# Layer 0's row sums folded into partition halves by DMA, and six graphs in the schedule instead of five

## The chip, the cores and the metric

The kernel runs on one core of one Trainium2 chip. The metric is the device time of one launch in microseconds. Engines are named as in the profile: PE is TensorE's matmul (PEld its weight load), DVE VectorE, ACT ScalarE, POOL GpSimd, SP SyncE. Each engine runs its own instructions in order and waits for others by semaphores; DMAs are issued from SP and from POOL.

## The reference

The input is 32 independent graphs of 512 nodes with 256 features (x is 32 x 512 x 256 in float32) and one 512 x 512 adjacency matrix. Four layers follow each other, each as `x = layernorm(x + layer(x))`:

- Layer 0: self-attention with 8 heads of 32 features, masked by the adjacency, then residual, layernorm, a two-product MLP with ReLU, residual and layernorm.
- Layer 1: graph attention with one head; the score is a leaky ReLU of a sum of a source and a target term.
- Layer 2: full attention with learned projections and a leaky ReLU on the scores, then ReLU.
- Layer 3: graph attention with 4 heads of 64 features, then ELU.

What matters here is the softmax of layer 0:

```
scores = einsum('fnhd,fmhd->fhnm', q, k) / sqrt(D)
scores = where(mask, scores, -1e9)
attn = softmax(scores, axis=-1)
t = einsum('fhnm,fmhd->fnhd', attn, v).reshape(F, N, C)
```

The kernel does not divide before the product with v: it computes the masked exponentials p, the product of p with v, and for each head and each node n the sum of p over m. The division comes after.

## The kernel before, in words

**Layout.** A tile of kind `p` is 128 partitions x 4 x 512 in float32 (8 KB per partition, 1 MB). In layer 0 the partitions are 128 of the 512 nodes m, the 4 parts are four heads (a head group), and the 512 columns are the nodes n. There are two head groups (g = 0, 1) and four node chunks (m = 0 to 3), so eight such tiles in each graph.

**Layer 0's attention (`layer0`, from L1046).** For each g and m: `exps` makes four score products that run on four row strips of TensorE (L1027) and four exponentials on ScalarE (L1031); VectorE multiplies by the mask (L1079); four products with v run on four column strips (L1086) and add up in one PSUM bank over m. `collect` (L1061 and after) sums the four chunks of a group outside TensorE: `add_dma` (L961 to L969) issues a DMA from POOL's queue that adds one tile to another in SBUF. For each group there are three: chunk 1 onto 0, chunk 3 onto 2, 2 onto 0. What is left is one tile for each group, kept in `totals`; its 128 partitions still have to be summed. `sums` (L1056, recorded at L1058) does it on TensorE: for each of the four parts a product whose stationary operand is `pick[:, g, :]`, a 128 x 32 tile that is zero but for a column g of ones. It runs on column strip j, so that row g of strip j of the bank `sm` becomes the row sum of head j of group g. The two groups take eight products. Each float32 product is two matmul instructions in the profile, so there are 16 for a graph. `rinv0` then moves `sm` back into columns and takes the reciprocal, and `heads_out` multiplies by it.

**Layer 3** does the same with four heads and its own sums (L1268); there `add_dma(total, None)` adds the second half of a tile's parts to the first. Its gates reach all partitions by way of DRAM: `gates` writes rows (L1173) and reads them back as a broadcast of 1 MB (L1179, `p<-row`) on SP's queue; layer 1 has a smaller one (`e<-row`). VectorE makes p from the broadcast at L1277 and masks it at L1284.

**The last graph** (`at_once`) takes the sums of all eight tiles on TensorE directly, without DMAs. `skip(n)` puts in n empty steps, so that every graph has the same number of steps.

**The schedule.** All 32 graphs are written as lists of steps (`plan(engine, ns, run, reads, writes, ...)`), each with an assumed duration. `Plan.place` (L521) then decides, in Python and before anything runs, in which order each engine issues the steps of all graphs: it keeps a clock for each engine, picks among the steps that are ready the one that can start first, and among those the one due first. A DMA's transfer is a step of a sixth engine, "DMA", with a `lag` until it has landed. The order is fixed in the program; at run time engines only wait for semaphores. What steers it:

- `WAYS`: a step of graph g may be placed only while g is less than WAYS past the oldest unfinished graph.
- `due` (L1351 and after): PACE times the graph's number plus a time from TENTHS (FIRST and LAST for the first four and last five graphs), by how far along the step is.
- `STAY`: a PE step whose mode of tiling differs from the last one's is treated as due later by this much. `tiling` is 1 for the row strips of the scores, 2 for the column strips of products with v and of sums, 3 for layer 3's products, 0 for the rest; `SWITCH` is the 100 ns that the planner charges for a change.
- `START`: the earliest time of the first graphs' first step.

Buffers are few and shared by all graphs (6 of kind x, 7 y, 3 v, 9 t, 8 p, 8 PSUM banks), and `place` gives them out as well.

Of the kernel before, what the change touches and what calls it, by code (L numbers as in the profile page):

```python
# [9 lines left out]
FP = mybir.dt.float32  # L10
# [7 lines left out]
P = 128  # L18
# [8 lines left out]
H0, H3 = 8, 4  # L27


WAYS = 5  # L30
PACE = 90.30
STAY = 4.86
START = (0, 0, 53.29, 88.61, 134.37)

TENTHS = (0, 26.21, 86.69, 92.24, 176.51, 212.02, 277.3, 313.49, 381.31, 382.21, 490.27)
FIRST = (
    (-14.58, 58.82, -25.93, -24.45, 99.53, 212.02, 277.3, 225.46, 380.43, 381.33, 489.39),
    (20.46, 79.82, -4.21, 95.49, 168.52, 212.02, 277.3, 315.61, 382.59, 384.58, 492.64),
    (10.74, 90.74, 6.57, 60.81, 176.51, 212.02, 277.3, 313.49, 383.92, 382.21, 492.29),
    (-115.77, 26.21, 86.69, 92.58, 176.51, 210.06, 277.3, 313.49, 381.31, 382.21, 487.12),)  # L40
LAST = (
    (0, 25.88, 86.52, 92.24, 176.3, 211.81, 277.09, 313.28, 381.68, 376.38, 536.57),
    (0, 27.77, 86.69, 92.22, 176.49, 212, 277.93, 316.39, 400.99, 521.01, 653.82),
    (0, 26.21, 87.61, 91.24, 177.97, 214.48, 309.58, 343.79, 765.5, 770.4, 888.75),
    (-0.65, 26.94, 85.87, 100.46, 141.72, 174.63, 259.04, 341.35, 397.71, 410.07, 514.93),
    (3.71, 25.72, 94.73, 50.65, 70.79, 101.96, 247.58, 292.79, 344.82, 346.48, 489.36),)
@with_exitstack
def general_path(
    ctx: ExitStack,
# [408 lines left out]
class Plan:  # L458
# [59 lines left out]
                live[slot.kind][r] += 1  # L518
        return live

    def place(self, urgency, ways, stay=0.0, run=True):  # L521


        held_by = {g: self.profile(g) for g in {op.graph for op in self.ops}}
        engines = {e: 0.0 for e in (PE, DVE, ACT, POOL, SP, DMA)}
        waiting = {e: [] for e in engines}
        free = {k: [(0.0, i) for i in range(n)] for k, n in self.counts.items()}
        todo, held = {}, {}
        for op in self.ops:
            todo.setdefault(op.graph, set()).add(op.rank)  # L530
            if not op.missing:
                waiting[op.engine].append(op)
        order, front, ended = sorted(todo), {g: 0 for g in todo}, {}
        port, port_by, end, tiling = 0.0, None, 0.0, 0
        self.trace = []

        def safe(op, kind, new):
            spare = len(free[kind]) - len(new)
            if spare < 0:
                return False  # L540
            have = spare
            for g in order:
                mine = held.get((g, kind), [])
                have += len(mine)
                if g == op.graph:
                    have += len(new)
                    mine = mine + new
                r, rows = front[g], held_by[g][kind]
                ahead = sorted(s.first for s in mine if s.first > r)
                for i, stop in enumerate(ahead + [len(rows)]):  # L550
                    if stop > r and max(rows[r:stop]) + len(ahead) - i > have:
                        return False
                    r = max(r, stop)
                if g == op.graph:
                    return True

        while todo:
            choice = None
            for e, ops in waiting.items():
                found = []  # L560
                for op in ops:
                    if order[0] + ways <= op.graph:
                        continue
                    due = urgency(op)
                    t = max(engines[e], op.ready, ended.get(op.graph - ways, 0.0))
                    if op.port and port_by is not e:
                        t = max(t, port)
                    if choice and t > choice[0]:
                        continue
                    wants = {}  # L570
                    for s in op.slots:
                        if s.index is None:
                            wants.setdefault(s.kind, []).append(s)
                    if all(safe(op, kind, new) for kind, new in wants.items()):
                        for kind, new in wants.items():
                            t = max(t, sorted(free[kind])[len(new) - 1][0])
                        if op.tiling != tiling and e is PE:
                            due += stay
                        found.append((t, due, op))
                if found:  # L580
                    best = min(found, key=lambda f: f[:2])
                    if choice is None or best[0] < choice[0]:
                        choice = best
            assert choice, "no instruction can be placed: too few buffers"
            t, _, op = choice
            if op.engine is PE and op.tiling != tiling:
                t, tiling = max(t, engines[PE] + SWITCH), op.tiling
            waiting[op.engine].remove(op)
            for s in op.slots:
                if s.index is None:  # L590
                    pick = min(free[s.kind])
                    free[s.kind].remove(pick)
                    s.index, s.graph = pick[1], op.graph
                    held.setdefault((op.graph, s.kind), []).append(s)
            engines[op.engine] = t + op.ns
            if op.port:
                port, port_by = t + op.ns, op.engine
            done = t + op.ns + op.lag + SIGNAL
            end = max(end, done)
            for s in op.slots:  # L600
                s.users -= 1
                s.ends = max(s.ends, done)
                if not s.users and s.kind:
                    free[s.kind].append((s.ends, s.index))
                    held[s.graph, s.kind].remove(s)
            for other in op.then:
                other.missing -= 1
                other.ready = max(other.ready, done if other.engine != op.engine or op.lag
                                  else t + op.ns)
                if not other.missing:  # L610
                    waiting[other.engine].append(other)
            left = todo[op.graph]
            left.remove(op.rank)
            while front[op.graph] not in left and left:
                front[op.graph] += 1
            ended[op.graph] = max(ended.get(op.graph, 0.0), t + op.ns + SIGNAL)
            if not left:
                del todo[op.graph]
                order.remove(op.graph)
            self.trace.append((t, op))  # L620
            if run and op.run:
                op.run()
        return end


def fast_path(
# [34 lines left out]
    nc = tc.nc  # L661
    B, N, C = x.shape
    NC = N // P
    KC = C // P
# [28 lines left out]
    ones = const.tile([P, P], FP, name="ones")  # L693
    nc.gpsimd.memset(ones, 1.0)

    pick = const.tile([P, 2, 32], FP, name="pick")
    nc.gpsimd.memset(pick, 0.0)
    for g in range(2):
        nc.gpsimd.memset(pick[:, g, g:g + 1], 1.0)


    fit = const.tile([P, NC * H0], FP, name="fit")
# [13 lines left out]
    def T(slot):  # L716
        return slot.tile if slot.kind is None else buffers[slot.kind][slot.index]
# [240 lines left out]
            [(s, c) for s in (a, b) if s is not None for c in (c0, c0 + 1)] + [row] * (row is not None),  # L958
            [(dst, c0), (dst, c0 + 1)])

    def add_dma(dst, src):  # L961

        def run():
            a, b = (T(dst), T(src)) if src else (T(dst)[:, 0:2, :], T(dst)[:, 2:4, :])
            nc.gpsimd.dma_start(a, b, accum_op=ALU.add)  # L965
        reads = [src, dst] if src else [dst]
        started = Slot(None)
        plan(POOL, 950, run, reads, [dst, started])
        plan(DMA, 5600 if src else 2650, None, reads + [started], [dst], lag=2500)  # L969
# [71 lines left out]
    def skip(n):  # L1041

        for _ in range(n):
            plan(DMA, 0, None)

    def layer0(xs, at_once):  # L1046
# [9 lines left out]
        def sums(g, p, start, stop):  # L1056
            for j in range(J):
                nc.tensor.matmul(T(sm)[j * 32:(j + 1) * 32, :], pick[:, g, :], T(p)[:, j, :],  # L1058
                                 start=start, stop=stop)
# [35 lines left out]
            totals.append(ps[0])  # L1095

        if at_once:
            skip(1)
        else:
            plan(PE, 1740, lambda: [sums(g, p, g == 0, g == KC - 1) for g, p in enumerate(totals)],  # L1100
                 totals, [sm], tiling=2)
        rinv = rinv0(sm)
        t = heads_out(oT, rinv, H0)

# [261 lines left out]
    with tc.manual_schedule(engines={mybir.EngineType.PE, mybir.EngineType.DVE,  # L1366
                                     mybir.EngineType.Activation, mybir.EngineType.Pool,
                                     mybir.EngineType.SP}):
        plan.place(urgency, WAYS, 1e3 * STAY)


    bad, col, total = buffers["rs"][:3]
# [51 lines left out]
```

## Time and profile before

The time is 2933.48 us, the median of three runs (2933.24 to 2937.47). The profiled execution has a span of 2933.2 us.

| what | value |
|---|---|
| TensorE (PE) | 2860.7 us busy, 98%, 14262 instructions |
| VectorE (DVE) | 2290.8 us, 78% |
| ScalarE (ACT) | 1888.0 us, 64% |
| GpSimd (POOL) | 953.7 us, 33% |
| DMA, POOL's queue | 292.57 MB, 49.7% of 16 engines |
| DMA, SP's queue | 80.49 MB, 9.0% of 16 engines |
| L1058, row sums of layer 0 | 560 instructions, 68.0 us busy |
| L965, accumulating DMAs | 310 issues, mean 882 ns each |

How to read it: the share is busy time over the span. A matmul's duration in the profile runs from its start to its modelled end, and several are in flight at a time, so the distance from one start to the next says more than the duration. In a group's line `out<-in` are the program's names, x is the count, then come the busy time and the mean of one, and last the idle time just before with what ended it. "Granted clock" is the share of TensorE's full clock.

### The profile page before, as it was taken

The numbers are of one execution on the slowest core, as the hardware profiler recorded it, in microseconds if no ns is written. First come the engines' busy times: TensorE is split into PE (matmuls) and PEld (weight loads), VectorE is DVE, ScalarE is ACT, GpSimd is POOL, SyncE is SP. The second block draws the span as 40 slices with busy tenths as digits, with TensorE's granted clock in tenths as the row PEclk, the third lists the DMA queues.
The fourth block names the chain that finished last, engine by engine and source line by source line (L and its number), as shares of the span: only waits on it lengthen the run. The fifth ranks groups of instructions, "written<-read, shape, count | busy, mean of one in ns | idle before, by whom it ended". The sixth has DMA issues, their size and how long they took to land.

```text
span 2933.2 us, 39746 instructions
## 1 busy us (share of the span) xinstructions
PE 2860.7 (98%) x14262; PEld 1586.7 (54%) x14262; DVE 2290.8 (78%) x4076; ACT 1888.0 (64%) x4104; POOL 953.7 (33%) x898
## 2 busy tenths in 40 slices
PE   8999999999999999999999999999999999999995
PEld 3455555555555555555555555555555555555572
DVE  5568887887878878778887778878778888777877
ACT  5665676666766667666667666667666667666653
POOL 0332233322333323433233343233433232333222
PEclk9999999999999999999999999999999999999998
DMA  6646665566655657556666556666556666555125
GB/s 164 133 83 137 132 132 125 110 150 135 143 122 110 148 126 151 119 113 139 141 147 142 128 115 137 143 145 140 130 115 137 143 145 139 131 113 125 48 59 126
DMA packets 93707, 375.66 MB, mean 128 GB/s; under 512 B 8768, under 2 KB 44736, under 8 KB 57664
## 3 DMA queue, kind: packets, MB, share of 16 engines
q0 software_dynamic: 44640, 292.57, 49.7%
q1 hardware_dynamic: 48864, 80.49, 9.0%
q8 instruction: 114, 1.87, 0.3%
q14 instruction: 89, 0.73, 0.1%
HBM read 63.38 MB, written 17.10 MB: 27 GB/s over the span
## 4 chain that ended last, share of the span: by engine, by line
PE 92%; DMA 3%; DVE 3%; ACT 1%; issue 1%; POOL 0%; DVEq 0%; SPq 0%; ACTq 0%
PE bank L924 15%; PE bank L910 11%; PE bank L1027 8%; PE bank L1086 8%; PE bank L1247 8%; PE bank L1293 8%; PE bank L1231 8%; PE bank L1208 8%; PE bank L897 5%; PE bank L1123 4%; PE bank L1135 3%; DMA p<-row 2%; PE bank L1058 2%; PE bank L1010 2%; DVE p L1079 1%; PE bank L978 1%
## 5 line engine op out<-in xcount | busy, mean ns | idle before, releaser
L965 POOL DMA_DIRECT2D p<-p x310 | 271.8, 882 | 1457.6 <-DMA p<-p 505.0
L1031 ACT ACTIVATE p<-bank 128x512 f32<-128x512 f32 x1024 | 546.7, 604 | 161.3 <-PE bank L1027 161.2
L1079 DVE TENSOR_TENSOR p<-p,edge_t 128x2048 f32<-128x2048 f32 x256 | 591.3, 2314 | 52.1 <-ACT p L1031 50.8
L885 ACT ACTIVATE t<-bank 128x512 f32<-128x512 f32 x640 | 369.1, 598 | 331.9 <-PE bank L1293 116.3
L955 POOL TENSOR_TENSOR y<-y,x 128x512 f32<-128x512 f32 x192 | 340.3, 1783 | 289.2 <-ACT y L1322 148.7
L938 DVE BATCH_NORM_STATS2 st<-y 128x6 f32<-128x256 f32 x768 | 314.0, 409 | 18.3 <-POOL y L955 11.5
L1086 PE MATMUL bank<-p,v 128*32 128x512 f32 x2048 | 277.3, 615 | 25.9 <-DVE p L1079 25.9
L1027 PE MATMUL bank<-t,t 32*128 32x512 f32 x2048 | 296.4, 643 | 0.0
L1284 DVE TENSOR_TENSOR p<-p,edge_t 128x2048 f32<-128x2048 f32 x128 | 293.1, 2290 | 3.3
L1277 DVE TENSOR_SCALAR p<-p,e,e 128x512 f32<-128x512 f32 x512 | 256.6, 545 | 36.4 <-DMA p<-row 36.0
L948 ACT ACTIVATE x<-y,rs,rs 128x256 f32<-128x256 f32 x512 | 270.9, 596 | 3.8 <-DVE rs L945 3.7
L1208 PE MATMUL bank<-v,p 128*128 128x257 f32 x1024 | 243.7, 385 | 3.5 <-issue 3.5
L910 PE MATMUL bank<-t,wqkv 128*128 128x512 f32 x512 | 240.7, 603 | 3.4 <-ACT t L885 3.3
L1247 PE MATMUL bank<-v,p 128*128 128x257 f32 x1024 | 242.3, 386 | 0.0
L1293 PE MATMUL bank<-p,v 128*64 128x512 f32 x1024 | 241.7, 613 | 0.5 <-DVE p L1284 0.5
L1231 PE MATMUL bank<-t,t 128*128 128x512 f32 x512 | 238.5, 599 | 0.0
L885 ACT ACTIVATE v<-bank 128x258 f32<-128x258 f32 (+2 forms) x384 | 172.1, 460 | 95.5 <-PE bank L924 92.8
L1247 PEld LDWEIGHTS bank<-v,p 128*128 128x128 f32 x1024 | 188.9, 190 | 64.5 <-ACT t L885 20.5
L1208 PEld LDWEIGHTS bank<-v,p 128*128 128x128 f32 x1024 | 190.3, 192 | 44.0 <-issue 18.2
L1027 PEld LDWEIGHTS bank<-t,t 32*128 32x128 f32 x2048 | 82.6, 184 | 163.3 <-issue 107.0
L939 DVE BATCH_NORM_AGGREGATE mv<-st 128x2 f32<-128x6 f32 x768 | 139.8, 182 | 26.3
L948 ACT ACTIVATE y<-y,rs,rs 128x256 f32<-128x256 f32 x256 | 140.0, 607 | 30.7 <-DVE rs L945 29.9
(120 smaller groups left out, 4167.3 us busy)
## 6 DMA issues: line engine op xcount, KB each, us to landing
p<-p POOLq DMA_DIRECT2D x248, 1024.0 KB, 7.5
p<-row SPq DMA_DIRECT2D x32, 1024.0 KB, 6.4
p<-p POOLq DMA_DIRECT2D x62, 512.0 KB, 4.6
x<-in_x_dram SPq DMA_DIRECT2D x32, 512.0 KB, 7.4
out_dram<-x SPq DMA_DIRECT2D x32, 512.0 KB, 2.9
e<-row SPq DMA_DIRECT2D x32, 256.0 KB, 3.1
t<-in_adj_dram SPq DMA_DIRECT2D x4, 256.0 KB, 6.2
wqkv<-in_L_gnn_w_qkv_dram SPq DMA_DIRECT2D x1, 768.0 KB
```

The costliest lines, as they stand in the source:

```text
L885: act(170 + n * 0.84, lambda: nc.scalar.activation(to(T(dst)), frm(T(src)), AF.Copy), [src], writes)
L910: nc.tensor.matmul(T(bank), T(w)[:, i, col:col + P], T(xT)[:, i, :], start=(i == 0), stop=(i == KC - 1))
L924: nc.tensor.matmul(T(bank)[:, j * width:(j + 1) * width], T(xT)[:, k, (c0 + j) * P:(c0 + j + 1) * P], T(w)[:, k, col:col + width], start=( ...
L948: act(600, lambda c=c: nc.scalar.activation(T(dst)[:, c, :], T(y)[:, c, :], AF.Identity, bias=T(nm)[:, c:c + 1], scale=T(rs)[:, c:c + 1]), ...
L1027: nc.tensor.matmul(T(banks[j]), T(kT)[r, g, m * P:(m + 1) * P], T(qT)[r, g, :], start=True, stop=True)
L1031: act(600, lambda j=j: nc.scalar.activation(T(p)[:, j, :], T(banks[j]), AF.Exp, scale=1.0 / math.sqrt(D0)), [banks[j]], [(p, j)])
L1079: dve(2420, lambda p=p, m=m: nc.vector.tensor_tensor(T(p), T(p), T(edge_t)[:, m, :].unsqueeze(1).to_broadcast([P, J, N]), ALU.mult), [p, ( ...
L1086: nc.tensor.matmul(T(av)[j * D0:(j + 1) * D0, :], T(v)[:, m, h * D0:(h + 1) * D0], T(p)[:, j, :], start=(m == 0), stop=(m == NC - 1))
L1208: nc.tensor.matmul(T(bank)[:, :C + 1], T(p)[:, m, c * P:(c + 1) * P], T(v)[:, m, 2:C + 3], start=(m == 0), stop=(m == NC - 1))
L1231: nc.tensor.matmul(T(bank), T(xT)[:, k, m * P:(m + 1) * P], T(qT)[:, k, :], start=(k == 0), stop=(k == KC - 1))
L1247: nc.tensor.matmul(T(bank)[:, :C + 1], T(p)[:, m, c * P:(c + 1) * P], T(v)[:, m, :C + 1], start=(m == 0), stop=(m == NC - 1))
L1293: nc.tensor.matmul(T(av)[i * D3:(i + 1) * D3, :], T(q)[:, m0 + m, 2 * H3 + h * D3:2 * H3 + (h + 1) * D3], T(p)[:, 2 * m + i, :], start=(m0 ...
```

## The change

It has two parts.

The first is in layer 0, for all graphs but the last. The two totals stay two tiles, `low` (group 0) and `high` (group 1). One accumulating DMA adds the upper 64 partitions of `low` to its lower 64, another adds the lower 64 partitions of `high` to its upper 64. Then a plain DMA on SP's queue copies the upper half of `high` to the upper half of `low`. `low` now has group 0 in partitions 0 to 63 and group 1 in 64 to 127. `pick` gets a third plane with ones in column 0 for the lower and in column 1 for the upper partitions, and four products with it (eight instructions) give the rows that eight products gave before. `skip(7)` replaces `skip(1)` for the last graph, because the other graphs now have six steps more.

The second is in the schedule: WAYS is 6 instead of 5, STAY is 0, PACE, START, TENTHS, FIRST and LAST have other values, and there is a new bound: no step may be placed earlier than EARLY (186.52 us) before it is due.

```diff
-WAYS = 5
-PACE = 90.30
-STAY = 4.86
-START = (0, 0, 53.29, 88.61, 134.37)
+WAYS = 6
+PACE = 81.87
+STAY = 0.00
+START = (0, 10.17, 59.24, 97.18, 85.64)
+EARLY = 186.52
...
-TENTHS = (0, 26.21, 86.69, 92.24, 176.51, 212.02, 277.3, 313.49, 381.31, 382.21, 490.27)
+TENTHS = (0, 35.72, 65.32, 68.92, 152.58, 202.32, 246.27, 266.73, 356.34, 362.66, 490.49)
...
                     t = max(engines[e], op.ready, ended.get(op.graph - ways, 0.0))
+                    if op.graph >= 0:
+                        t = max(t, due - early)
...
-    pick = const.tile([P, 2, 32], FP, name="pick")
+    pick = const.tile([P, 3, 32], FP, name="pick")
     nc.gpsimd.memset(pick, 0.0)
     for g in range(2):
         nc.gpsimd.memset(pick[:, g, g:g + 1], 1.0)
+        nc.gpsimd.memset(pick[g * 64:(g + 1) * 64, 2, g:g + 1], 1.0)
...
-    def add_dma(dst, src):
+    def add_dma(dst, src, halves=None):
...
-            a, b = (T(dst), T(src)) if src else (T(dst)[:, 0:2, :], T(dst)[:, 2:4, :])
+            a, b = (T(dst), T(src)) if src else halves(T(dst)) if halves else (
+                T(dst)[:, 0:2, :], T(dst)[:, 2:4, :])
...
         if at_once:
-            skip(1)
+            skip(7)
         else:
-            plan(PE, 1740, lambda: [sums(g, p, g == 0, g == KC - 1) for g, p in enumerate(totals)],
-                 totals, [sm], tiling=2)
+            low, high = totals
+            add_dma(low, None, lambda t: (t[:64], t[64:]))
+            add_dma(high, None, lambda t: (t[64:], t[:64]))
+            started = Slot(None)
+            plan(SP, 450, lambda: nc.sync.dma_start(T(low)[64:], T(high)[64:]), totals, [low, started])
+            plan(DMA, 1300, None, totals + [started], [low], lag=2500)
+            plan(PE, 870, lambda: sums(2, low, True, True), [low], [sm], tiling=2)
```

## The prediction

> **What bounds the kernel now.** I read the page from the top: busy shares, the chain of waits, then the costliest groups.
>
> ```profile
> span 2933.2 us, 39746 instructions
> PE 2860.7 (98%) x14262; PEld 1586.7 (54%) x14262; DVE 2290.8 (78%) x4076; ACT 1888.0 (64%) x4104; POOL 953.7 (33%) x898
> ...
> PE 92%; DMA 3%; DVE 3%; ACT 1%; issue 1%; POOL 0%; DVEq 0%; SPq 0%; ACTq 0%
> ```
>
> TensorE is busy for 98% of the span and is 92% of the chain that ended last; VectorE is next with 78%. So a product taken off TensorE counts, and work added elsewhere counts only where TensorE comes to wait for it. Is it equally full everywhere? I cut the run into two equal windows between start and tail, and added the two ends:
>
> ```profile
> 400.00:1400.00 1000.00, 981.02 (x4889) 543.81 (x4890) 785.58 (x1386) 651.97 (x1420) 341.41 (x312) 0.99 0.61 131
> 1400.00:2400.00 1000.00, 999.64 (x5017) 554.48 (x5016) 806.72 (x1423) 672.15 (x1464) 343.91 (x315) 1.00 0.63 137
> 0.00:200.00 200.00, 182.81 (x902) 90.01 (x903) 118.60 (x206) 116.44 (x235) 45.11 (x54) 0.96 0.61 134
> 2600.00:2933.00 333.00, 301.64 (x1474) 172.31 (x1470) 261.69 (x496) 191.62 (x425) 96.33 (x89) 0.96 0.40 92
> ```
>
> The second column is TensorE. The 14262 matmul instructions less 46 of set-up and check and 72 that the last graph has extra (64 instead of 16 row-sum instructions in layer 0, 32 instead of 8 in layer 3) are 442 per graph. So the first window does 4889/442 = 11.06 graphs, 90.4 us each; the second 11.35, 88.1 us each. The second window has no hole left: 88.1 us is what TensorE's own work takes. The first loses 2.3 us per graph; over the some 14 graphs that run before 1400 us that is 32 us. Start and tail leave TensorE idle for 17 and 31 us. The waits of TensorE and of VectorE say what makes the first window slower:
>
> ```profile
> PE bank L1086 <- DVE p L1079: 25.9, 13, 4.4
> PE bank L1380 <- DVE rs L1377: 11.3, 1, 11.3
> ...
> DVE p L1277 <- DMA p<-row: 36.0, 11, 6.2
> ```
>
> (Columns: total us, times, longest.) VectorE stands at L1277 for layer 3's gate broadcast (`p<-row`, 1 MB). Its queue is in order, the layer 0 mask L1079 is behind it, and TensorE's attention product L1086 waits for that mask. The timeline has this at 511 to 518 us and about every second graph up to 1260: that broadcast took 10.3 us beside two accumulating DMAs, TensorE waited 3.9 us, and the granted clock in the next 20 us was 0.93.
>
> Now the row sums themselves, in the stretch of the timeline around one of them:
>
> ```profile
> 1511.06 1.07 PE L1086 MATMUL bank<-p,v 128*32 128x512 f32 x8
> ...
> 1516.47 1.88 PE L1231 MATMUL bank<-t,t 128*128 128x512 f32 x4
> 1518.18 3.60 PE L910 MATMUL bank<-t,wqkv 128*128 128x512 f32 x8
> ...
> 1528.64 1.92 PE L1058 MATMUL bank<-p,pick 128*32 128x512 f32 x16
> 1530.49 1.98 PE L910 MATMUL bank<-t,wqkv 128*128 128x512 f32 x4
> ```
>
> Starts tell more than durations, which overlap. L1058 holds TensorE from 1528.64 to 1530.49: 1.85 us for 16 instructions, which run in four waves of four column strips. Four full instructions of L1231 take 1.71 us, 0.43 each; so a wave costs what one full instruction costs.
>
> [...] start to start, a 512-column instruction takes 429 ns inside a mode and 523 ns where the next is of another mode, so 94 ns per change (L1086's eight above: 1.00 us up to the next start at 1512.06, against two waves of 0.43). [...] No run here has a half-partition transfer[...]. [...] `p<-row` lands in 6.4 us by the median and in 10.3 beside two adds. [...]
>
> **The change, part by part.**
>
> *Row sums of layer 0.* For graphs 0 to 30, 16 instructions become 8: two waves fewer, 2 x 0.43 = 0.86 us, with the few ns between instructions 0.9. 31 x 0.9 = **28 us off TensorE**, in every window, because TensorE is the bound in all of them. The last graph takes its sums at once and keeps its 64.
>
> *The fold chain.* Each of those graphs gets two accumulating half-partition DMAs (512 KB) on POOL's queue and one SP copy (512 KB); the sums wait for the copy.
>
> ```profile
> p<-p POOLq DMA_DIRECT2D x248, 1024.0 KB, 7.5
> p<-p POOLq DMA_DIRECT2D x62, 512.0 KB, 4.6
> out_dram<-x SPq DMA_DIRECT2D x32, 512.0 KB, 2.9
> ```
>
> Fold: 4.6 us from issue to landing, if half the partitions cost nothing; at most 1.7 + 2 x 2.9 = 7.5 us, if the part that grows with size (7.5 - 4.6 = 2.9 us for 512 KB) doubles. Copy: 2.9 us by `out_dram<-x`[...]. In the stretch above the last add of that graph starts at 1517.5 and lands (by the median) at 1525.0; the sums start 3.6 us later. After the change: fold, 1529.6 to 1532.5; copy with 0.33 us of issue, 1532.8 to 1537.3, thus 7.8 to 12.3 us after the add. The planner charges 950 + 2650 + 2500 + 450 + 1300 + 2500 and three signals of 70, 10.6 us, and places the sums by that, beyond the 3.6 us that its 9.1 us for an add (7.5 measured) already leaves. Spare: 3.6 + 10.6 - (7.8 to 12.3) = 1.9 to 6.4 us. I take the fold at 5.5, the copy at 3.5, and no wait on TensorE; a fold that collides as the broadcast does could cost a few us in single graphs.
>
> *Queues.* POOL: 62 more issues of 0.87 us, 54 us on an engine 33% busy; behind a waiting fold stand other graphs' adds and the y additions, which have the same spare. SP: 31 issues of 0.33 us; but SP then waits in order for both folds, and behind it stand the gate rows and broadcasts (L1173, L1179), the x load and the store. A fold that is late by d delays a broadcast just behind it by up to d, and VectorE waits for broadcasts. Six such instructions per 88 us make that rare. DMA share: 49.7% for 292.57 MB on POOL's queue and 9.0% for 80.49 MB on SP's give 5.5 + 1.8 points for 32.5 and 16.3 MB more: 59% becomes 66%. Buffers: two of the eight `p` tiles are held some 10 us longer per graph, 20 of 704 buffer-us; hidden while other graphs have products ready. All this at 0 in the likeliest case.
>
> *STAY to 0.* It gave ops of the mode that runs a bonus of 4.86 us. I counted 32 changes of mode per graph in the second window; 22 tiled groups each standing alone would make 44. With no bonus a tiled group follows another by chance in 22 of 74 ops, and two in five of those are of the same mode: 44 - 6.5 x 1.4 = 35. Three more by 94 ns by 32 graphs: **+9 us**. Ends: 0, and 12 x 0.094 x 32 = +36. I take +8.
>
> *Six ways, EARLY, START, due times.* No instruction is added. Graph g+6 instead of g+5 must wait for graph g's end, so the sixth may start (by EARLY, 81.87 x 5 - 186.5 = 223 us) before the first ends. More ready products can fill holes: first window up to 32 us, start and tail perhaps 10 of their 48. But x, v, p and t buffers are the same number, and another order can make new holes as the old made the period-two ones. The trace cannot show it. Bounds: -42 to +50; I take a quarter of the 32, **-8 us**.
>
> Sum: 2933.2 - 28 + 8 - 8 = **2905 us**. The profiled span equals the median of the other runs, 2933.48, so nothing is converted.
>
> **Rivals.**
> 1. *Six graphs fill everything.* First window at the pace of the second (-32), half the mode changes' cost (+4), 28 off: 2877. For it: five ways with graphs in flight for 490 of 90 us is more than five. Against: unchanged buffers, and holes that come from DMA latency, not from lack of graphs.
> 2. *Slower: the broadcast stall spreads.* Three more transfers per graph and an SP queue that waits make the L1277 wait as regular in the rest of the run as it is before 1400: 18 more graphs by 2.3 us, 41, and 8 for modes, less 28: 2954. It decides from 28 - 8 = 20 us of additional waiting, 0.65 us per graph. For it: one wait of 3.9 us every second graph already does more. Against: with the same broadcasts the second window shows almost none.
> 3. *Slower through modes alone.* All 44 changes: 2933.2 - 28 + 36 = 2941. It decides from 28/(32 x 0.094) = 9.3 more changes per graph; the ops need to avoid each other for that.
> 4. *No change:* new waits of about 20 us give it all back, 2933. That the sums are not halved I exclude: a wave's cost follows its 512 columns, and one stationary with two columns of ones sums both halves.
>
> **How the numbers follow.** Likeliest case 0.53 (2885 to 2924), rival 1 0.22, rival 2 0.14, rival 3 0.05, rival 4 0.06. Faster by over 0.2% (about what a measurement of this kernel can tell from no change): 0.53 + 0.22 = 0.75; within: 0.06; slower: 0.14 + 0.05 = 0.19. Range 2872 to 2945: leaves out the lower edge of rival 1 and most of rival 2.
>
> **What would show it.** L1058's successor: 312 instructions instead of 560 (31 x 8 + 64), about 0.95 us for each eight. The full-pace window near 87.4 us per graph. No TensorE wait at the sums; if there is one, the fold chain was priced too low. Folds landing in 4.6 to 7.5 us. 33 to 37 mode changes per graph. The L1086 wait behind L1277 in fewer graphs than before; in more, rival 2 is right. DMA share about 66%. The prediction is wrong if TensorE's total wait in the middle grows by over 20 us, or if start or tail lose more than 30.

## The result and the profile after

The changed kernel takes **2893.86 us** (median of 4 runs, 2891.89 to 2894.81) against 2933.62 for the kernel before: a ratio of 0.9861, 95% interval 0.9844 to 0.9878, 40 us less. The forecast was 2905, 28 us less, with a range of 2872 to 2945.

Head and chain from the page of the kernel after:

```profile
span 2891.7 us, 39629 instructions
PE 2832.4 (98%) x14014; PEld 1579.2 (55%) x14014; DVE 2443.2 (84%) x4076; ACT 1885.5 (65%) x4104; POOL 865.9 (30%) x962
...
PE 92%; DVE 3%; DMA 2%; issue 1%; ACT 1%; POOL 0%; SPq 0%; ACTq 0%; DVEq 0%; POOLq 0%
```

TensorE has 248 instructions fewer (31 x 8) and is still the bound. VectorE has the same 4076 instructions but 152 us more of busy time, which no step of the prediction had; 123 us of it come with the new order alone (2413.8 us in the run of experiment 4, which has neither folds nor copy). The stretches, cut as before (columns: stretch, length, then busy time and count for PE, PEld, DVE, ACT, POOL; granted clock, DMA share, GB/s):

```profile
400.00:1400.00 1000.00, 998.76 (x4953) 559.22 (x4950) 879.30 (x1433) 671.11 (x1459) 305.26 (x343) 1.00 0.73 154
1400.00:2400.00 1000.00, 998.35 (x4986) 561.96 (x4988) 877.28 (x1435) 674.42 (x1477) 307.56 (x345) 1.00 0.73 154
0.00:200.00 200.00, 175.04 (x853) 84.75 (x853) 116.61 (x201) 113.87 (x230) 46.64 (x60) 0.97 0.76 162
2560.00:2893.00 333.00, 300.70 (x1437) 168.56 (x1433) 267.33 (x497) 189.16 (x420) 92.34 (x92) 0.96 0.42 94
```

A graph now has 442 - 8 = 434 instructions, so the first stretch does 11.41 graphs, 87.6 us each (90.4 before), and the second 11.49, 87.0 us each (88.1 before). The first stretch is now as full as the second. The start has lost 8 us of TensorE's busy time (182.8 before), and the tail is as it was. The waits of TensorE and of VectorE that answer to those shown of before:

```profile
PE bank L1093 <- DVE p L1086: 9.7, 6, 2.7
...
DVE p L1290 <- DMA p<-row: 1.0, 2, 0.6
```

The wait on the gate broadcast is gone (36.0 us before), and with it the 4 us waits of TensorE.

**A balance to compare runs by.** I gave each matmul instruction its usual distance to the next start (429 ns for 512 columns, others in proportion to their columns, as the trace of before has 216 ns for 256 and 109 for 128; a wave of strips, whose starts are 6 to 7 ns apart, as one; 94 ns for a change of mode). The sum is TensorE's work; the rest of the span is holes, slower clock, first and last moments, and what an instruction takes beyond this charge. So only the differences between kernels tell something. From the traces, in us, with the changes of mode:

| kernel | work | rest | span |
|---|---|---|---|
| before (1032 changes of mode) | 2731 | 202 | 2933 |
| after (1038) | 2705 | 187 | 2892 |

So 26 us of the gain is work and 15 is rest. The experiments take these two apart.

### The profile page after: what moved, and what is told of

It is laid out like the page before. It is cut to its first block, busy times and chain, and to the rows that moved or that the text cites. A ratio compares the mean times of both kernels' runs of the same rounds, so it can differ in the third digit from the quotient of the medians.

```text
span 2891.7 us, 39629 instructions
## 1 busy us (share of the span) xinstructions
PE 2832.4 (98%) x14014; PEld 1579.2 (55%) x14014; DVE 2443.2 (84%) x4076; ACT 1885.5 (65%) x4104; POOL 865.9 (30%) x962
## 3 DMA queue, kind: packets, MB, share of 16 engines
q0 software_dynamic: 49600, 325.08, 57.2%
q1 hardware_dynamic: 51344, 96.75, 11.6%
## 4 chain that ended last, share of the span: by engine, by line
PE 92%; DVE 3%; DMA 2%; issue 1%; ACT 1%; POOL 0%; SPq 0%; ACTq 0%; DVEq 0%; POOLq 0%
PE bank L929 15%; PE bank L915 11%; PE bank L1034 9%; PE bank L1093 8%; PE bank L1306 8%; PE bank L1221 7%; PE bank L1244 7%; PE bank L1260 7%; PE bank L902 5%; PE bank L1136 4%; PE bank L1148 4%; PE bank L1017 2%; DMA p<-p 1%; PE bank L1281 1%; PE bank L1065 1%
## 5 line engine op out<-in xcount | busy, mean ns | idle before, releaser
L972 POOL DMA_DIRECT2D p<-p x372 | 322.3, 871 | 1787.8 <-DMA p<-p 568.4
L1086 DVE TENSOR_TENSOR p<-p,edge_t 128x2048 f32<-128x2048 f32 x256 | 618.2, 2424 | 59.7 <-ACT p L1038 59.5
L1038 ACT ACTIVATE p<-bank 128x512 f32<-128x512 f32 x1024 | 537.9, 599 | 89.2 <-PE bank L1034 87.6
L1290 DVE TENSOR_SCALAR p<-p,e,e 128x512 f32<-128x512 f32 x512 | 331.3, 680 | 1.0 <-DMA p<-row 1.0
L960 POOL TENSOR_TENSOR y<-y,x 128x512 f32<-128x512 f32 x192 | 273.7, 1432 | 158.2 <-ACT y L1265 100.1
L1297 DVE TENSOR_TENSOR p<-p,edge_t 128x2048 f32<-128x2048 f32 x128 | 304.9, 2382 | 2.2
L1034 PE MATMUL bank<-t,t 32*128 32x512 f32 x2048 | 302.6, 644 | 0.0
L953 ACT ACTIVATE x<-y,rs,rs 128x256 f32<-128x256 f32 x512 | 277.6, 596 | 24.6 <-DVE rs L950 24.3
L1221 PE MATMUL bank<-v,p 128*128 128x257 f32 x1024 | 237.8, 381 | 0.7 <-DVE p L1214 0.4
L890 ACT ACTIVATE v<-bank 128x264 f32<-128x264 f32 (+2 forms) x384 | 176.5, 460 | 90.2 <-PE bank L929 88.3
L1260 PE MATMUL bank<-v,p 128*128 128x257 f32 x1024 | 227.4, 380 | 0.0
L1244 PE MATMUL bank<-t,t 128*128 128x512 f32 x512 | 225.1, 592 | 0.0
L1034 PEld LDWEIGHTS bank<-t,t 32*128 32x128 f32 x2048 | 86.0, 184 | 169.5 <-issue 101.5
L902 PE MATMUL bank<-ident,x 128*128 128x128 f32 x1024 | 148.9, 279 | 11.7 <-DMA x<-in_x_dram 7.7
```

Source lines behind the costliest of these rows:

```text
L890: act(170 + n * 0.84, lambda: nc.scalar.activation(to(T(dst)), frm(T(src)), AF.Copy), [src], writes)
L1034: nc.tensor.matmul(T(banks[j]), T(kT)[r, g, m * P:(m + 1) * P], T(qT)[r, g, :], start=True, stop=True)
L1038: act(600, lambda j=j: nc.scalar.activation(T(p)[:, j, :], T(banks[j]), AF.Exp, scale=1.0 / math.sqrt(D0)), [banks[j]], [(p, j)])
L1086: dve(2420, lambda p=p, m=m: nc.vector.tensor_tensor(T(p), T(p), T(edge_t)[:, m, :].unsqueeze(1).to_broadcast([P, J, N]), ALU.mult), [p, ( ...
L1221: nc.tensor.matmul(T(bank)[:, :C + 1], T(p)[:, m, c * P:(c + 1) * P], T(v)[:, m, 2:C + 3], start=(m == 0), stop=(m == NC - 1))
L1244: nc.tensor.matmul(T(bank), T(xT)[:, k, m * P:(m + 1) * P], T(qT)[:, k, :], start=(k == 0), stop=(k == KC - 1))
```

## The experiments

The kernel before, measured beside each of them, had a median of 2931 to 2934 us; the differences below are against that one.

**1. Can the parts be tried by planning anew?** Four kernels, ordered by the kernel's own planner from their lists of steps. First the kernel before with half of the row-sum products; its list of steps is unchanged, and so is its order:

```diff
-            plan(PE, 1740, lambda: [sums(g, p, g == 0, g == KC - 1) for g, p in enumerate(totals)],
+            plan(PE, 1740, lambda: sums(2, totals[1], True, True),
```

> The kernel before, in its old order, with 8 of the 16 row-sum instructions per graph taken away and nothing put in their place (group 1's tile is summed into both rows, so group 0's row sums are left out). Theory (TensorE is the bound in every stretch, the sums' time comes off in full): 31 x 0.9 = 28 us less, 2905 to 2907. Rival (in the first 1400 us the period-two wait on the gate broadcast sets the pace, so time taken off TensorE there only lengthens the wait): only the second half's 15 graphs gain, about 14 us, 2919.

It took 11868 us: the values left the range that the fast path checks at its end, and the general path ran as well. It says nothing on the sums; experiment 2 repeats it without that.

Then the fold chain with the five schedule values of before:

```diff
-WAYS = 6
+WAYS = 5
...
-EARLY = 186.52
+EARLY = 1e9
```

(and PACE, STAY, START, TENTHS, FIRST, LAST of before)

> The fold chain with the schedule values of before (five ways, STAY 4.86, old due times, no EARLY). Theory (sums and schedule are two separate gains, 27 and 14 us): about 2906, with holes in the first 1400 us as before. Rival 1 (the new transfers collide with the gate broadcast when the schedule is not made for them): slower than the half-products run, 2920 to 2960. Rival 2 (the order is so sensitive that any replanning removes the old pattern): about 2895.

The new schedule values with the old sums:

```diff
-            add_dma(low, None, lambda t: (t[:64], t[64:]))
...
-            plan(PE, 870, lambda: sums(2, low, True, True), [low], [sm], tiling=2)
+            skip(6)
+            plan(PE, 1740, lambda: [sums(g, p, g == 0, g == KC - 1) for g, p in enumerate(totals)],
+                 totals, [sm], tiling=2)
```

> The new schedule values (six ways, EARLY, STAY 0, new due times) with the old 16 row-sum instructions and no folds. Theory (schedule worth 14 us by itself): about 2920. Rival (the schedule gain exists only with the fold chain, because p tiles and DMA were tuned together): 2933 or slower.

And the changed kernel with `WAYS = 5`:

> The changed kernel with WAYS 5 and all else new. If the sixth graph in flight is what closes the holes between 400 and 1400 us: holes there come back, 2915 to 2930. If the due times and START did it: within 5 us of the changed kernel's 2894.

These three took 3304, 5471 and 3115 us: ratios of 1.127 (1.125 to 1.129), 1.866 (1.863 to 1.869) and 1.062 (1.060 to 1.064). No theory had that. TensorE's waits in the second of the four, then the stretch 400 to 1400 us of the fourth:

```profile
PE bank L1093 <- DVE p L1086: 156.2, 58, 6.8
...
400.00:1400.00 1000.00, 955.00 (x4633) 517.16 (x4632) 770.25 (x1333) 627.10 (x1363) 334.78 (x316) 0.99 0.67 143
```

58 waits of TensorE for VectorE's masks where the kernel before has 13; 45 us of holes in 1000 us. A few steps more, or one graph fewer in flight, and the same due times give quite another order. I read this as values that fit one list of steps only. So these runs do not say what a part is worth, and the fourth does not show that the sixth graph alone closes the holes. Everything that follows keeps the order of every engine as it was and changes only what a step emits.

**2. Half the row-sum products in the old order.** The edit of the first kernel above, with the range check kept from calling the general path.

> The kernel before, in exactly its old order on every engine, with 8 of the 16 row-sum instructions per graph taken away and nothing in their place; group 0's row sums are left out, and the range check at the end is kept from calling the slow general path. Theory (the sums' time comes off in full, in every stretch): 31 x 0.9 = 28 us less, 2905. Rival (in the first 1400 us the wait on the gate broadcast sets the pace, so what is taken off TensorE there lengthens the wait): only the later graphs gain, 14 us, 2919.

2889.1 us, ratio 0.9859 (0.9842 to 0.9875): 42 us less, more than either theory. By the balance, work is 2705 (27 less, about as expected) and rest 182 (20 less).

**3. The broadcast.** The kernel before in its old order, with layer 3's gate broadcast cut to a quarter:

```diff
-            to = lambda: flat(T(G))
+            to = lambda: flat(T(G))[:, :4 * P]
...
-            to(), T(row)[:R, :].rearrange("r q -> (r q)").partition_broadcast(P)),
+            to(), T(row)[:min(R, 4), :].rearrange("r q -> (r q)").partition_broadcast(P)),
```

> The kernel before in exactly its old order, with layer 3's gate broadcast cut from 1 MB to 256 KB per graph (three of four heads' gates are left as what the buffer held). Theory (the holes before 1400 us come from this broadcast landing late beside the accumulating DMAs): they close, 26 to 32 us less, 2901 to 2907, and the stretch 400 to 1400 us is as full as 1400 to 2400. Rival (VectorE's queue is late there for another reason and the broadcast is only what it stands at): under 8 us.

2907.9 us, ratio 0.9919 (0.9902 to 0.9935), 24 us less. The two stretches and the wait:

```profile
400.00:1400.00 1000.00, 997.94 (x5019) 553.16 (x5018) 806.86 (x1419) 671.91 (x1463) 346.29 (x318) 1.00 0.60 127
1400.00:2400.00 1000.00, 999.41 (x5007) 556.78 (x5007) 805.43 (x1425) 666.40 (x1450) 347.36 (x318) 1.00 0.59 126
...
PE bank L1086 <- DVE p L1079: 9.5, 11, 2.7
```

With no other change the first stretch holds 5019 instructions instead of 4889 and is as full as the second. So the holes before 1400 us were the broadcast's late landing, as the prediction read them; my 32 us for them was some 8 too many, because I had charged 14 graphs, also those before 400 us, where the smaller broadcast saves nothing.

Both edits together tell whether experiment 2's extra 14 us are the same holes.

> The kernel before in its old order, with both edits: 8 of 16 row-sum instructions per graph taken away, and the gate broadcast cut to 256 KB (group 0's row sums and three heads' gates are left out). The first edit alone gave 42 us, the second 24. Theory (the 14 us that the first gave beyond its 28 us are the same holes before 1400 us as the second closed): 2931 - 28 - 24 = about 2880. Rival (two separate gains): 2931 - 42 - 24 = 2866.

2878.5 us, ratio 0.9819 (0.9803 to 0.9836): the same holes. In the trace of before they are five waits of 3.1 to 4.4 us at 518, 700, 881, 1062 and 1243 us, at a spacing of about 181 us, two graphs. In experiment 2, 0.9 us less work per graph leaves two of over 1 us between 400 and 1400 us, of 1.5 and 2.9, and one of 4.0 later. I read this as a coincidence of transfers that keeps its phase and that a small shift breaks; no run moved the phase alone.

**4. The new order with the old sums.** The changed kernel, order kept, without folds and copy, and with 16 row-sum instructions:

```diff
         def run():
+            if halves:
+                return
...
-            plan(SP, 450, lambda: nc.sync.dma_start(T(low)[64:], T(high)[64:]), totals, [low, started])
+            plan(SP, 450, lambda: None, totals, [low, started])
...
-            plan(PE, 870, lambda: sums(2, low, True, True), [low], [sm], tiling=2)
+            plan(PE, 870, lambda: [sums(0, low, True, False), sums(1, low, False, True)], [low], [sm], tiling=2)
```

> The changed kernel in exactly its new order on every engine, with 16 row-sum instructions per graph as before and without the two folds and the copy (both sums read the same tile, so group 1's row sums are left out; range check held as in the run above). Theory (the two gains are separate and the folds cost TensorE nothing): 2894 + 28 = 2922, and 11 to 12 us under the kernel before. Rival (folds and copy hold TensorE up somewhere, so part of the 28 us is eaten): less than 2922, by what they cost.

2912.4 us, ratio 0.9936 (0.9919 to 0.9953): **the order alone gives 19 us** against before. The first stretch is full without any halved sum:

```profile
400.00:1400.00 1000.00, 998.83 (x5033) 556.33 (x5033) 860.35 (x1415) 664.69 (x1446) 285.59 (x321) 1.00 0.62 136
```

But from here to the changed kernel are 19 us (21, if each is taken against the kernel before that was measured beside it) and not 28, so some 7 to 9 us are eaten.

**5. What eats them?** First without SP's copy, folds kept (`lambda: None` in its place):

> The changed kernel in its new order with both folds but without SP's copy (rows 64 to 127 of the first tile stay group 0's, so group 1's row sums are left out). The changed kernel stands 18 us under the run with old sums and no DMAs, where the products alone are worth 28: about 9 us are eaten by folds and copy. If SP's copy eats them (the sums later, SP blocked): 2885 to 2887. If the folds do[...]: 2893 to 2895.

2896.3 us (0.9868 to 0.9901 of before), no gain over the changed kernel: it is not the copy, nor SP's waiting. Then the folds cut to 4 KB each, still 64 rows and as many issues:

```diff
-            add_dma(low, None, lambda t: (t[:64], t[64:]))
-            add_dma(high, None, lambda t: (t[64:], t[:64]))
+            add_dma(low, None, lambda t: (t[:64, 0, :16], t[64:, 0, :16]))
+            add_dma(high, None, lambda t: (t[64:, 0, :16], t[:64, 0, :16]))
```

> The run before without SP's copy (2896), and its two folds cut from 512 KB to 4 KB each, with the same number of rows and issues on POOL in the same places (group 1's row sums are left out). It tells apart how the folds take some 10 us from TensorE. Theory A (VectorE is held up[...]): no gain, 2892 to 2897, and VectorE's gate op L1290 stays near 670 ns. Theory B (the bytes: DMA share, later landings, POOL waiting for them): 2883 to 2887, and L1290 may still be slow or not.

2895.5 us (0.9858 to 0.9891): not the bytes either, though the DMA share fell from 0.73 to 0.63. And the control, 8 products with neither folds nor copy:

> The changed kernel's order with its 8 row-sum instructions per graph, but with no folds and no copy at all (group 0's and group 1's sums are the same, group 1's are left out). The control to the run with tiny folds (2895) and to the one with old sums and no folds (2912). Theory (POOL's 62 more issues cost the 10 us by holding VectorE): 2912 - 28 = 2884. Rival (the folds cost nothing; a shorter TensorE alone uncovers small waits on the others in this order): 2893 to 2896.

2887.7 us, ratio 0.9848 (0.9832 to 0.9865), between the two theories. The balance of these runs:

| kernel, all in the new order | work | rest | median us |
|---|---|---|---|
| old sums, no folds, no copy | 2732 | 180 | 2912.4 |
| 8 products, no folds, no copy | 2705 | 181 | 2887.7 |
| 8 products, tiny folds, no copy | 2705 | 186 | 2895.5 |
| 8 products, folds, no copy | 2705 | 187 | 2896.3 |
| the changed kernel | 2705 | 187 | 2893.9 |

A shorter TensorE uncovers 1 to 2 us. The 62 issues on POOL cost 5 to 6 us by the traces. By the medians, each against the kernel before that was measured beside it, they cost 4 to 8 us; the interval of the control overlaps that of the changed kernel and that of the tiny folds, so the size rests on the traces. Bytes and copy cost nothing that shows. VectorE's gate op in the last control, and then with tiny folds (columns: count, busy us, mean ns, idle before):

```profile
L1292 DVE TENSOR_SCALAR p<-p,e,e 128x512 f32<-128x512 f32 x512 | 298.6, 617 | 0.6 <-DMA p<-row 0.6
...
L1290 DVE TENSOR_SCALAR p<-p,e,e 128x512 f32<-128x512 f32 x512 | 325.9, 670 | 2.0 <-DMA p<-row 2.0
```

The median of one is 540 ns in both kinds of run; the mean goes up because a few are held (up to 2.4 us). So with 62 more issues on POOL VectorE's ops are held longer. But TensorE does not pay at these. It runs the same 14014 instructions in the same order in the control and in the three kernels with folds, so the distances from start to start can be compared one by one. TensorE's last start is 4.7 to 6.3 us later with folds, and the score products L1034 alone add 4.7 to 5.7 us. A moment of the changed kernel's timeline shows how:

```profile
587.79 1.14 PE L1034 MATMUL bank<-t,t 32*128 32x512 f32 x8
...
587.89 0.82 POOL L972 DMA_DIRECT2D p<-p  x1 [1.18 <-DMA p<-p]
588.04 2.00 DVE L950 SCALAR_TENSOR_TENSOR rs<-mv,rs 128x4 f32<-128x4 f32 x1 [1.46 <-ACT rs L948]
588.45 1.56 POOL L960 TENSOR_TENSOR y<-y,x 128x512 f32<-128x512 f32 x1
...
590.08 0.60 ACT L953 ACTIVATE x<-y,rs,rs 128x256 f32<-128x256 f32 x1 [2.07 <-DVE rs L950]
590.58 2.04 ACT L1038 ACTIVATE p<-bank 128x512 f32<-128x512 f32 x4
590.78 2.04 PE L1034 MATMUL bank<-t,t 32*128 32x512 f32 x8
```

Read from the top: POOL waits 1.18 us for an add to land and then issues a fold; its next instruction, the addition L960, comes that much later and falls beside L950. L950 works on four columns (the same op took 0.15 us at 500.74 in the trace before). Here it lasts 2.00 us and ends with POOL's addition. ScalarE stands 2.07 us for it, its exponentials L1038 come late, and the eight score products that need the banks these free take 2.04 us, where the eight at 587.79 took 1.14. In the control POOL goes on to the addition without a fold; it ends 0.12 us after L950's start instead of 1.97, and L950 takes 0.16 us.

After the first 200 us the changed kernel has eight such holds, of 1.4 to 2.0 us, each with a fold's issue just before the addition; tiny folds have nine, folds without the copy eight. The score products behind them lose 4.9, 5.5 and 4.6 us against the control, of 4.9, 4.7 and 6.3 us that the folds cost there in all. This account is read from the traces; no run moved the addition alone. In the trace L950 ends with POOL's addition, at 590.04 and 590.01 us; but at 588.04 it had begun before that addition (588.45), though after the issue (587.89). What holds it there is not shown by any run.

**6. How much room has the fold chain?** The changed kernel with SP's copy done twice, the second after the first has landed:

```diff
-            plan(SP, 450, lambda: nc.sync.dma_start(T(low)[64:], T(high)[64:]), totals, [low, started])
+            plan(SP, 450, lambda: [nc.sync.dma_start(T(low)[64:], T(high)[64:]) for _ in range(2)], totals, [low, started])
```

> The changed kernel in its new order with SP's half-tile copy done twice, the second waiting for the first to land: about 4 us later sums in each of 31 graphs, SP blocked as much longer, 16 MB more traffic. Theory (1.9 to 6.4 us are to spare at the sums): TensorE waits little, under 1 us per graph on the mean, 2894 to 2915. Rival (the sums stand right at the landing of the copy): about 4 us per graph come on top, 2990 or more.

2923.5 us, ratio 0.9973 (0.9963 to 0.9982), 30 us over the changed kernel: more than my theory, yet not by the rival's way. From the first to the second copy are 4.2 to 4.5 us in most graphs, and from the second to the sums still a median of 10.7 us. The waits of TensorE and the window at the start:

```profile
PE bank L1065 <- DMA p<-p: 15.9, 2, 14.2
...
100.00:200.00 100.00, 77.59 (x378) 40.09 (x375) 53.40 (x95) 50.51 (x108) 32.21 (x31) 0.89 0.70 138
```

One wait of 14.2 us, at the first graph's sums, where little other work is there yet, with the clock down to 0.89 in that stretch. After 200 us the sums wait 0.9 us in all. Some 12 us are spread over the stretch 400 to 2400, and they have another place. TensorE's waits for ScalarE at L985 in the changed kernel, then with the copy twice, and ScalarE's line with the copy twice:

```profile
PE bank L985 <- ACT e L890: 1.9, 3, 0.7
...
PE bank L985 <- ACT e L890: 12.9, 22, 1.6
...
L953 ACT ACTIVATE x<-y,rs,rs 128x256 f32<-128x256 f32 x512 | 277.8, 596 | 88.2 <-DMA out_dram<-x 60.7
```

ScalarE stands 60.7 us, in 26 waits, for the store of x to land, which it never does in the changed kernel, and TensorE comes to wait behind it. In 24 of these 26 graphs the store is issued within 0.02 us of what it waits for, so SP does not make it late. But the second copy is issued only 0.6 to 2.9 us before the store, where in the changed kernel the one copy is 4.2 to 7.0 us ahead. So I read it as the second transfer beside the store rather than SP's stand; no run tested this alone.

## Why the prediction was right, and where it was off

- **The row sums: right.** L1065 has 312 instructions, as forecast. Two pairs of runs differ in little but the 248 instructions and have few holes: 29 us between the two runs of experiment 3, 25 us in the new order without folds. 28 was forecast; experiment 2's 42 us are 28 and the 14 of the holes.

```profile
L1065 PE MATMUL bank<-p,pick x312: 589/593/617, 103.5 to 2684.0; 128*32 128x512 f32 x156
```

- **"No wait on TensorE" at the sums: right, with more room than I worked out.** This is the same place in the timeline of after, SP's copy and the sums:

```profile
1492.31 0.47 SPq L1112 DMA_DIRECT2D p<-p  x1
...
1507.13 1.07 PE L1065 MATMUL bank<-p,pick 128*32 128x512 f32 x8
```

14.8 us, which is also the median of the 31 graphs; less 4.3 for the copy, 10.5 us are to spare, against 1.9 to 6.4 worked out. TensorE waits there once, 1.1 us, at the first graph. I had taken the place of the sums from the old order and the planner's charge; the new order simply puts them later. The fold's bounds of 4.6 to 7.5 us, the upper one on my assumption, which nothing before showed, that the part that grows with size doubles, held for the middle: by shape in the trace the half-partition folds land in 5.1 (shortest) and 7.1 us (median), where I took 5.5; the copy's 4.3 is more than the 3.5 that I took. The late end of the copy's range, 1537.3 us, and with it the 12.3 and the 1.9 us of room, allowed the copy more than that, which no trace of before showed.

- **STAY to 0, "+8 us": wrong.** There are 1038 changes of mode in the run where there were 1032, 0.6 us. The estimate assumed that tiled groups meet by chance; under the new due times they stand together about as often as under the bonus.

- **"A quarter of the 32" for the schedule, -8 us: the term that was mis-sized.** The order alone gave 19 us (experiment 4). It closed all of the holes before 1400 us, which are worth 24 (experiment 3), and gave some back at the start. This is rival 1's main step, which had 0.22; what kept the time from 2877 were the start (the order's own: 175 us of TensorE's busy time in the first 200 without folds too) and the next point. In hindsight the old holes were five coincidences of one broadcast, and in experiment 2 a shift of 0.9 us in each graph broke most of them: a reason to expect them to go rather than a quarter of them. That the new order is a good one could not be read from the trace, as the prediction says itself: its +50 us on the slow side is not worked out there, and in experiment 1 slightly different steps or ways made the order 181 to 2538 us slower. To that extent the range held by luck.

- **The fold chain's queues "at 0": wrong by some 5 us.** The prediction had the place: behind a waiting fold stand "the y additions, which have the same spare". They have room for themselves, but moved about 1 to 2 us they fall beside a tiny op of VectorE, and ScalarE and TensorE wait behind that (experiment 5). I counted POOL's 54 us of issues against POOL's own idle time, and named who waits in POOL's queue but not who is held on another.

- **The slower rivals did not come.** The broadcast wait (rival 2) fell to 1.0 us; the DMA share rose somewhat more than forecast, without harm (57.2 + 11.6 + 0.3 = 69% for 66).

The errors: 8 us of modes not lost, the schedule 11 better than taken, folds some 5 worse. Together they leave the time some 11 us below the forecast, within the few us to which these terms are known.

## What to carry to other kernels

Where a planner fixes the order, a part of a change is tried by keeping the order and changing what a step emits; planning anew with the same values moved the time by 6 to 87% here and tells nothing about the part. The regular hole every second graph was one cause here, a late transfer: price such a hole as one thing that goes or stays rather than by a share. And a DMA issued from POOL is not free because POOL is idle (62 more cost 5 to 6 us here): ask which of POOL's instructions it moves, what they will run beside on VectorE, and who waits for that.

## What the hardware showed that I had not expected

- 62 more DMA issues on POOL, with 4 KB each, raised the mean of VectorE's 128 x 512 scalar op from 617 to 670 ns, and the kernel took about as long as with 62 of 512 KB (2895.5 and 2896.3 us).
- An op on 128 x 4 elements lasted 2.00 us beside POOL's work, where it took 0.15 in the trace of before (experiment 5). Eight such holds account for the 5 us that the folds cost on TensorE, two engines further on.
- A copy of 512 KB between partition halves of SBUF took 4.2 to 4.5 us from issue to the next issue that waits for it in experiment 6, where a full-partition store of 512 KB landed in 2.9 in the trace of before.
